# Differential attention on one core: the output tile is copied out of PSUM by ScalarE and normed in SBUF

## The chip, the cores and the metric

The kernel runs on one core of a Trainium2 chip. The core has five engines, each with a queue of its own that it works through in order: TensorE (PE in the profile, its weight loads PEld), VectorE (DVE), ScalarE (ACT), GpSimd (POOL) and SyncE (SP), which issues the DMAs. Matrix products are written to PSUM, eight banks of 2 KB in each of 128 partitions; everything else lives in SBUF. The metric is the device time of one execution in microseconds (us).

## The reference, cut to what matters

Four sandwiched layers are computed on x of 8 sequences of 512 tokens of 256 features, each as x = x + layernorm(layer(layernorm(x))): differential attention, a local transformer, token and channel diffusion, and a mixture of experts. Only the end of the first one is touched:

```python
attn = softmax(A1) - lam * softmax(A2)        # causal, 16 heads
O = einsum('bhnm,bhmd->bhnd', attn, V)
O = O / rms * rms_scale * (1.0 - LAMBDA_INIT)
Oc = O.transpose(0, 2, 1, 3).reshape(b, n, H * 2 * dh)
return Oc @ Wo.T                              # y
...
x = x + _layernorm(y, axis=-1)                # (y - mean) / sqrt(var + 1e-5)
```

The change concerns the last two lines: the product with Wo, its norm, and the addition to x.

## The kernel before, in words

The differential attention is the function `diff`, the first stage of the kernel. It works through 64 turns n: 8 sequences, 4 groups of 4 heads in each, and 2 softmaxes for each group. A turn has 8 slots, and the loop over slots at the end of `diff` writes the order of everything by hand:

- In each slot, TensorE makes a pair of score blocks `sc` (L355) for the row maxima of turn n, and a pair of transposed blocks `sa` (L365) for the exponentials of an earlier turn. The four products use different quarters of the array's rows and run together. VectorE adds a mask to `sc` (L368) and takes maxima into `spread` (L369); ScalarE makes the exponentials `e` from `sa` (L372); GpSimd masks one block of `e` in every second slot (L375, the selects).
- `lower` (slot 0): four transposes turn the maxima into `pm` (L288), and VectorE adds them to the queries `qT` (L380). The `sa` from slot 2 on need this `qT`.
- `divide` (slot 1): `pn` (L406) sums the exponentials, ScalarE makes the reciprocal `rec` (L408, L409), VectorE multiplies `oc` by it (L410); in every second turn VectorE joins the two softmaxes (L413) and GpSimd squares the result, `sq` (L415).
- `values` (slots 2 to 4): the products `po` with the values (L388), three additions of exponentials on GpSimd (L393), which together take some 7 us, and the copy of `po` to `oc` (L397, L399).
- `queries` and `keys` (slots 5 and 6 of every second turn), and `between()`, which does one part of the work waiting in a list: a sequence's `prepare`, a group's `heads` (`pr`, `rs`, and on GpSimd `oT`, L428), or a tile of a sequence's `finish`.

`finish` is what is changed. It has four tiles of 128 tokens, each done by one call of `between()`: `pp` is the product with Wo, in one PSUM bank; `self.norm` takes its statistics on VectorE (`st`, L184, and `mv`, L186), makes `rs` on GpSimd (L172, L173), and on VectorE makes `z` (L194); GpSimd adds `z` to `x` (L444). The tiles of one sequence fall into three successive turns: tile 0 at the end of the first, tiles 1 and 2 at the end of the second, tile 3 at the end of the third. `pp` shares a pool of two banks with most other products of the stage:

```python
psm, pse, ps = (pool(n, b, space=PSUM) for n, b in (("d_psm", 2), ("d_pse", 1), ("d_ps", 2)))
```

`pp`, `pm`, `pn`, `po`, `pr`, `pq`, `pk` and `pv` all take turns in the two banks of `d_ps`. So `pm` or `pn`, which follow `pp` at once, wait for the bank of a `pp` until its last reader has ended. `z` has two buffers in SBUF.

Of the kernel before, what the change touches and what calls it, by code (L numbers as in the profile page):

```python
# [120 lines left out]
class Net:  # L121
# [169 lines left out]
    def diff(self, nb):  # L291
# [4 lines left out]
        with ExitStack() as ctx:  # L296
            pool = lambda n, b, **k: ctx.enter_context(self.tc.tile_pool(name=n, bufs=b, **k))
            wk, small = pool("d_wk", 2), pool("d_small", 4)
            psm, pse, ps = (pool(n, b, space=PSUM) for n, b in (("d_psm", 2), ("d_pse", 1), ("d_ps", 2)))
            nc = self.nc  # L300
# [117 lines left out]
            def heads(m, oc, sq):  # L418

                b, r = divmod(m, 4)  # L420
                if r == 0:
                    outs[b] = wk.tile([P, 4, S], F32, name="oT", tag="oT")
                pr = ps.tile([P, S], F32, name="pr", tag="ps")
                self.mm(pr, [(self.const[:, C_B32:C_B32 + P], sq)])
                rs = wk.tile([P, S], F32, name="rs", tag="rs", bufs=1)
                nc.scalar.activation(rs, pr, AF.Ln, bias=column(C_EPS))
                nc.scalar.activation(rs, rs, AF.Exp, scale=-0.5)
                nc.gpsimd.tensor_mul(outs[b][:, r, :], oc, rs)  # L428
                if r == 3:
                    between.add(finish(b))  # L430
                return
                yield

            def finish(b):
                oT = outs.pop(b)
                for t in range(NT):
                    if t:
                        yield
                    pp = ps.tile([P, D], F32, name="pp", tag="ps")
                    self.mm(pp, [(oT[:, c, self.tok(t)], self.wo[:, c, :]) for c in range(4)])  # L440
                    z = wk.tile([P, D], F32, name="z", tag="z")
                    self.norm(small, [pp], [z])
                    xs = self.xb(b)[:, t, :]
                    nc.gpsimd.tensor_add(xs, xs, z)  # L444

# [1111 lines left out]
```

## Time and profile before

| | |
|---|---|
| median of 3 runs | 3858.41 us (3852.4 to 3862.06) |
| the profiled execution | 3852.22 us, of which the span 3850.4 us |
| mean granted TensorE clock | 0.955 of full speed |
| busy, share of the span | PE 90%, DVE 57%, ACT 48%, POOL 41% |
| the steady part of `diff`, 57 to 1146 us | 1089 us, PE busy 1027.9 us, POOL 716.0 us, granted clock 0.97 |
| `pp` read for the statistics (L184), 32 times | 0.43 us each |
| `z` from `pp` (L194), 32 times | 0.54 us each |

The span runs from the first to the last instruction. In the views an arrow reads "written from": `z<-pp,mv,rs` is the instruction that writes z from pp, mv and rs. A row of the timeline has its start, its length, engine, line, operation, operands, and in brackets how long the engine was idle before it and what it waited for. A group of like instructions that lie together is one row, marked x8 or the like.

### The profile page before, as it was taken

What the parts mean: (1) busy time and instruction counts of PE and PEld (TensorE: products, weight loads), DVE (VectorE), ACT (ScalarE), POOL (GpSimd) and SP (SyncE); (2) the same over time, 40 slices, a digit from 0 to 9 for tenths busy, and PEclk for the clock granted to TensorE, in tenths of its full rate; (3) what the DMA queues carried; (4) which work ended last, traced back from release to release, by engine and by line L of the source; (5) the groups of instructions that cost most, each with busy time, mean ns of one, the idle gap of its engine ahead of it and who ended that gap; (6) DMA issues with size and microseconds to landing.
All of it is one profiled execution on the core that took longest, in us unless ns stands there. A gap on an engine that the chain in (4) does not pass through costs nothing. (4 is left out here: it accounts for less than half of the span.)

```text
span 3850.4 us, 53540 instructions
## 1 busy us (share of the span) xinstructions
PE 3463.0 (90%) x20034; PEld 1885.2 (49%) x20034; DVE 2209.5 (57%) x4364; ACT 1840.8 (48%) x3687; POOL 1583.2 (41%) x1432
## 2 busy tenths in 40 slices
PE   8999999999987999999999999997988888679985
PEld 3344434343424556666666555564444444346554
DVE  6777767776646666665556666663244443344445
ACT  3555555555543444444444444453655555223334
POOL 3676666676654433333333333321012211153333
PEclk9999999999979999999999999998999999789997
DMA  9300000000001000000010000000000000421115
GB/s 343 124 1 7 7 6 1 7 6 1 6 6 34 4 4 4 4 4 25 4 31 12 9 9 9 9 20 23 1 23 23 23 17 17 146 70 53 52 44 166
DMA packets 95137, 130.28 MB, mean 34 GB/s; under 512 B 24702, under 2 KB 73242, under 8 KB 94874
## 3 DMA queue, kind: packets, MB, share of 16 engines
q1 hardware_dynamic: 88346, 108.94, 8.8%
q0 software_dynamic: 6528, 17.87, 1.3%
q8 instruction: 162, 2.65, 0.3%
q14 instruction: 101, 0.83, 0.1%
HBM read 57.40 MB, written 65.18 MB: 32 GB/s over the span
## 5 line engine op out<-in xcount | busy, mean ns | idle before, releaser
L372 ACT ACTIVATE e<-sa 128x1024 f32<-128x1024 f32 (+3 forms) x512 | 359.2, 702 | 337.3 <-PE sa L365 334.7
L393 POOL TENSOR_TENSOR e<-e,e 128x1536 f32<-128x1536 f32 (+2 forms) x192 | 451.6, 2352 | 92.4 <-PE po L388 82.5
L365 PE MATMUL sa<-qT,kT 32*128 32x512 f32 (+3 forms) x2048 | 430.0, 496 | 9.1 <-ACT e L372 8.8
L369 DVE TENSOR_REDUCE spread<-sc 128x2 f32<-128x256 f32 (+3 forms) x512 | 422.4, 825 | 15.6
L355 PE MATMUL sc<-kT,qT 32*128 32x128 f32 (+3 forms) x2048 | 420.3, 491 | 8.9 <-DVE spread L369 5.3
L655 ACT ACTIVATE lp<-lp,lnm 128x256 f32<-128x256 f32 (+1 forms) x512 | 240.1, 470 | 260.6 <-DVE lnm L647 156.2
L659 POOL TENSOR_TENSOR lp<-lp,lrs 128x1024 f32<-128x1024 f32 x64 | 121.1, 1893 | 528.8 <-DVE lrs L656 508.7
L1087 ACT ACTIVATE te<-tsa 128x1024 f32<-128x1024 f32 x256 | 249.0, 1024 | 136.6 <-PE tsa L1083 87.5
L368 DVE TENSOR_TENSOR sc<-sc,const 128x256 f32<-128x256 f32 x512 | 218.6, 427 | 158.6 <-PE sa L365 138.2
L355 PEld LDWEIGHTS sc<-kT,qT 32*128 32x128 f32 x2048 | 159.5, 188 | 282.9 <-issue 126.2
L213 PE MATMUL lpa<-ghT,lw 128*128 128x512 f32 x640 | 284.8, 600 | 12.1 <-ACT ghT L568 12.1
L213 PE MATMUL lqk<-qkv,lhT 128*128 128x512 f32 x512 | 247.8, 622 | 2.3 <-DVE qk L606 1.6
L607 POOL TENSOR_TENSOR qk<-qk,over 128x1024 f32<-128x1024 f32 x64 | 151.4, 2365 | 207.7 <-DVE qk L606 207.7
L375 POOL TENSOR_SCALAR_AFFINE_SELECT e<-e 128x512 f32<-128x512 f32 x256 | 160.4, 640 | 169.3 <-ACT e L372 169.3
L1406 ACT ACTIVATE ehT<-eht,enorm 128x128 f32<-128x128 f32 x288 | 108.2, 457 | 210.0 <-PE eht L1402 202.7
L213 PEld LDWEIGHTS lpa<-ghT,lw 128*128 128x128 f32 x640 | 119.4, 190 | 163.3 <-issue 136.3
L388 PE MATMUL po<-e,v 128*32 128x512 f32 (+3 forms) x2048 | 188.3, 451 | 4.0 <-POOL e L375 3.6
L644 DVE TENSOR_TENSOR lp<-lsc,const 128x768 f32<-128x768 f32 (+1 forms) x128 | 138.7, 1083 | 86.5 <-PE lsc L641 86.0
L641 PE MATMUL lsc<-lkT,lqT 64*128 64x256 f32 (+1 forms) x1024 | 156.6, 386 | 28.1 <-DVE qk L606 28.0
L365 PEld LDWEIGHTS sa<-qT,kT 32*128 32x128 f32 x2048 | 158.9, 189 | 43.4 <-ACT e L372 27.4
L1083 PE MATMUL tsa<-tqT,tkT 32*128 32x512 f32 x1024 | 171.0, 673 | 6.3 <-DVE tqT L1038 3.4
L213 PE MATMUL py<-ew,ehT 128*128 x576 | 145.2, 396 | 24.1 <-ACT ehT L1406 23.7
(293 smaller groups left out, 6799.5 us busy)
## 6 DMA issues: line engine op xcount, KB each, us to landing
xrows<-zero SPq DMA_DIRECT2D x66, 514.0 KB
ex<-xrows SPq DMA_DIRECT2D x72, 128.5 KB
ew<-in_L_ffn_w_dram SPq DMA_DIRECT2D x16, 512.0 KB
egot<-yrows SPq DMA_DIRECT2D x16, 512.0 KB
x<-in_L_attn_X_dram SPq DMA_DIRECT2D x8, 512.0 KB
saved<-x SPq DMA_DIRECT2D x8, 512.0 KB
lx<-saved SPq DMA_DIRECT2D x8, 512.0 KB
xf<-xf SPq DMA_DIRECT2D x8, 512.0 KB
```

Source lines behind the costliest of these rows:

```text
L213: self.nc.tensor.matmul(out, lhsT=l, rhs=r, start=i == 0, stop=i == len(pairs) - 1)
L355: nc.tensor.matmul(sc[:, i, :w], lhsT=qT[g, self.tok(t)], rhs=kT[g, :w], start=True, stop=True)
L365: nc.tensor.matmul(sa[:, i, :S - k * P], lhsT=kT[g, self.tok(k)], rhs=qT[g, k * P:], start=True, stop=True)
L368: nc.vector.tensor_add(sc[:, :, w - P:w], sc[:, :, w - P:w], own)
L369: nc.vector.tensor_reduce(self.spread[n % 2][:, t, g0:g0 + 2, 0 if n % 2 else 16], sc[:, :, :w], AX.X, ALU.max, negate=True)
L372: nc.scalar.activation(x[:, h0:h0 + 2, :], sa[:, :, :S - k * P], AF.Exp, scale=0.25)
L375: nc.gpsimd.affine_select(x[:, :, :P], x[:, :, :P], [[0, 4], [1, P]], ALU.is_ge, 0.0, base=0, channel_multiplier=-1)
L388: nc.tensor.matmul(pos[n][group(g), k * P:], lhsT=seqs[b][1][:, k, 4 * r + g, :], rhs=x[:, g, :], start=k == 0, stop=k == 2)
L393: nc.gpsimd.tensor_add(y, y, es.pop((n, k)))
L655: nc.scalar.activation(x, x, AF.Exp, bias=nm[:, i, k:k + 1], accum_out=rs[:, i, k:k + 1])
L1083: m = nc.tensor.matmul(sa[i // 2][:, i % 2, :], lhsT=kT[q, self.tok(k)], rhs=qT[q, :], start=True, stop=True)
L1087: nc.scalar.activation(e[:, 2 * i:2 * i + 2, :], sa[i], AF.Exp)
```

## The change

`finish` now copies `pp` to `z` on ScalarE. The norm then reads z and writes it in place, with the same instructions as before on VectorE and GpSimd. The bank's only reader is the copy.

```diff
                     z = wk.tile([P, D], F32, name="z", tag="z")
-                    self.norm(small, [pp], [z])
+                    nc.scalar.copy(z, pp)
+                    self.norm(small, [z], [z])
                     xs = self.xb(b)[:, t, :]
                     nc.gpsimd.tensor_add(xs, xs, z)
```

## The prediction

> **What bounds the kernel now.** I read, in this order: the table of windows, to see what the differential stage lacks; who waits for the tile z; and the timeline of one sequence's finish, twice.
>
> ```profile
> 57.00:1146.00 1089.00, 1027.94 (x7500) 428.88 (x7502) 747.43 (x1276) 591.70 (x913) 716.00 (x597) 0.97 0.08 29
> ```
>
> Columns: stretch, length, busy time of TensorE, its weight loads, VectorE, ScalarE, GpSimd; granted clock. TensorE is busy 1027.9 of 1089 us, so the stage runs at its pace: only TensorE's gaps and its clock (0.97, not 1) can be gained.
>
> ```profile
> who waited for it (us, times):
>   PEld pn L406: 28.0, 21
>   PE pn L406: 23.5, 21
>   POOL x L444: 21.1, 32
>   PEld pm L288: 9.0, 6
>   PE pm L288: 7.9, 6
> ```
>
> Of TensorE's gaps some 33 us are waits for z: pn 23.5 and pm 7.9 in TensorE's own rows, and 1.7 of pp's at the end. All come from the bank that pp holds until z is made. But such a sum is an upper bound: what is next late has to be looked up.
>
> Tiles 0 and 3 of each finish look like this (first sequence):
>
> ```profile
> 253.01 0.43 DVE L184 BATCH_NORM_STATS2 st<-pp 128x6 f32<-128x256 f32 x1 [0.77 <-PE pp L213]
> ...
> 254.91 0.54 DVE L194 TENSOR_SCALAR z<-pp,mv,rs 128x256 f32<-128x256 f32 x1 [0.58 <-POOL rs L173]
> 255.37 0.68 DVE L380 TENSOR_TENSOR qT<-qT,pm 128x512 f32<-128x512 f32 x1
> ...
> 255.50 1.07 PE L406 MATMUL pn<-e,const 128*32 128x512 f32 x8 [1.08 <-DVE z L194]
> ...
> 256.51 0.70 PE L365 MATMUL sa<-qT,kT 32*128 32x512 f32 x2
> ...
> 259.64 1.04 POOL L415 TENSOR_TENSOR sq<-oc 128x512 f32<-128x512 f32 x1 [2.79 <-DVE oc L413]
> ```
>
> The statistics start at 253.01, GpSimd makes rs, z ends at 255.45, and pn, which needs the bank, starts 1.07 us late. Behind z on VectorE stands qT (L380, ends 256.05), for which the next sa waits; and pn leads by rec and oc to sq, the start of GpSimd's next stretch. Tiles 1 and 2, a pass later:
>
> ```profile
> 260.64 7.20 POOL L393 TENSOR_TENSOR e<-e,e 128x1536 f32<-128x1536 f32 x3
> ...
> 268.98 1.27 POOL L428 TENSOR_TENSOR oT<-oc,rs 128x512 f32<-128x512 f32 x1
> ...
> 271.21 0.54 DVE L194 TENSOR_SCALAR z<-pp,mv,rs 128x256 f32<-128x256 f32 x1 [3.04 <-POOL rs L173]
> ...
> 271.81 0.33 PE L288 MATMUL pm<-const,spread 128*128 128x128 f32 x1 [1.32 <-DVE z L194]
> ...
> 272.12 0.69 DVE L369 TENSOR_REDUCE spread<-sc 128x2 f32<-128x512 f32 x1
> ...
> 272.88 0.90 PE L288 MATMUL pm<-const,spread 128*128 128x128 f32 x3 [0.74 <-DVE spread L369]
> ...
> 275.11 1.93 PE L406 MATMUL pn<-e,const 128*32 128x512 f32 x8 [0.59 <-DVE z L194]
> ...
> 276.99 1.22 PE L365 MATMUL sa<-qT,kT 32*128 32x512 f32 x2
> ```
>
> GpSimd runs without a gap from sq to oT and only then makes rs, so z waits 3.04 us, the maximum over scores (L369) stands behind z on VectorE, and TensorE idles for pm 1.32 us (the bank) and 0.74 us (the maximum). Then the clock is granted at half: pn takes 1.93 us here, 1.07 at tile 0; the pair sc and sa starts at 276.99 and po only at 279.00, 2.01 us later, against 1.06 at tile 0 (256.51 to 257.57).
>
> **The change, part by part.** Per tile one copy of 128x256 is added on ScalarE, 32 in all; bn_stats and the final tensor_scalar read SBUF instead of PSUM. Every engine's queue keeps its order, but for two places: the copy stands right behind the exponential of the slot before pp, and at tile 1 VectorE's sc add (L368) now stands ahead of z, not behind it.
>
> *The copy.* The page has none of 128x256. Bounds: the exponential of 128x256 from PSUM, 0.38 us, and the copy of 128x512, 0.58. I take 0.38, the same size. Behind it in ScalarE's queue waits the next exponential, behind that the next sa: but ScalarE idles 1.12 us (tile 0) and 1.43 and 1.76 us (tiles 1, 2) there, since sa is issued after pp. So the queue costs nothing; if that cover were gone, 0.38 x 32 = 12 us. The copy itself waits for pp and, as z has two buffers, for GpSimd's addition (L444) of the tile two before, which at tile 2 ended at 256.26, long ago. With two handovers of about 0.04 (pp's end 252.97 to the statistics 253.01) the statistics start 0.45 us later.
>
> *z and statistics from SBUF.* bn_stats: 0.41 (st<-x) against 0.43: nothing. The tensor_scalar: 0.41 in x<-x,mv,rs, 0.54 from PSUM; but h<-x,mv,rs, the same form, takes 0.40 to 1.36 while GpSimd adds. At z GpSimd has just made rs, and its next instruction waits for z, so it is idle: I take 0.41, a gain of 0.13; the upper end is 1.36.
> The Trainium skill, "SBUF — State Buffer", section "Who interferes with whom", speaks against the change here: a tensor_scalar in a 2-port mode and a GpSimd instruction exclude each other for a whole instruction. The spread of h agrees; if z always met such an instruction, the sum would be that of the slower rival below.
>
> *Tiles 0 and 3.* pn no longer waits, and starts 1.07 us earlier. But sa waits for qT: +0.45 - 0.13 makes its end 256.37 and sa 256.41 instead of 256.51. So of 1.07 us only 0.10 is left; the wait has moved from the bank to VectorE's queue. This holds for 12 tiles of sequences 0 to 5 and two of sequence 6.
> What else comes early is oc (L410, 257.93): rec no longer holds it, VectorE does: qT starts 0.32 later, then add (0.59), maximum (0.46) and its 0.43, so oc at 257.18, 0.75 earlier. So sq, the additions L393, the selects, oT and rs, back to back on GpSimd, move by 0.75.
>
> *Tile 1.* z at 270.46 instead of 271.21. From z's start to the maximum's was 0.91 us; the sc add between (0.46) now stands ahead, and z is 0.13 shorter: 0.32. The maximum starts at 270.78 instead of 272.12, and pm goes on 1.34 earlier, at 271.54. The bank itself is free long before. TensorE's idle time falls from 2.06 us to about 0.8 us. A gap of 1.07 at tile 0 leaves the clock whole, so I take it that 0.8 does.
>
> *Tile 2.* From the maximum to qT was 2.85 us on VectorE, now 2.72: qT 273.50 to 274.18, sa at 274.22 instead of 276.99. TensorE is ready before that: from pm's rest at 271.54 it is 0.48 to the next sc (as at full clock in sequence 1), 0.60 to pn and 1.0 for pn (as in turns with no finish beside): 273.62. So here too qT decides. At full clock po follows 1.06 us after sa, at 275.28 instead of 279.00: 3.72 us, and 0.15 more in the next slot (1.17 us against 1.0). So 3.87 us, tile 0 of this finish contained.
>
> *Sum.* The half clock lasts two windows (6.8 us) in sequences 0, 2, 4, 5 and one (3.4 us) in 1 and 3, where z of tile 1 to po takes 7.42 us instead of 7.79: 3.45 us there. 4 x 3.87 + 2 x 3.45 = 22.4. Tile 3, 6 x 0.10 = 0.6. Sequence 6: 2 x 0.10, and its last tile, where pm's rest (1066.05) hangs on two maxima behind z: z earlier by 0.75, add and z shorter by 0.59, so at 1064.5: 1.5. The last sequence, at the stage's end, has its four z in a chain with nothing beside: 4 x 0.13 less, one hop of 0.45 more: 0.1. Together 24.8 us. Later slots follow at the pace they have now, so nothing gives it back. The profiled execution took 3852.2 us, 6.2 under the median of the runs: 3827.4, in terms of the median 3833.6. I say 3833.
>
> **Rivals.**
> *The half clock stays.* It would, if its windows come from the low load around pm rather than from the 2.06 us. Then pm's rest costs 0.90 from 271.54 on, sc follows at 272.36, pn at 273.2, sc and sa at 275.05, po at 277.06 instead of 279.00: 1.94 x 6 = 11.6, with the other 2.4 us 14 us: 3844. For it: some idle time remains. Against: the half clock comes in each of these six places and after none of the gaps of 1.07 us.
> The Trainium skill, "TensorE: Matmul & The Clock Gate", section "Part 1: The HAM clock gate", gives a free-running window of about 3.4 us, and idleness of a whole window as what halves the clock; by that rule the gaps here would not be the cause and this rival would hold. The trace differs: 2.06 us in two parts were enough.
>
> *The wait only moves.* GpSimd's stretch does not move (oc held by something else) and the maximum stays behind a z that waits for rs: then TensorE starts each slot as before. About 3856. For it: tiles 0 and 3, where just that is forecast. Against: at tile 1 the sc add leaves z's shadow anyway.
>
> *Slower: z becomes the slow one.* Place: z in VectorE's queue ahead of qT. Price: at 1.36 us instead of 0.41, sa starts 0.85 late at 14 tiles (12 us), the four z of the end cost 3.8 more, and of the six turns perhaps 0.8 each is left (5 us): +11, 3869. It decides from about 1.1 us for z. Against it: GpSimd waits for z at that time.
>
> **How the numbers follow.** Forecast 0.70, half clock 0.15, moved wait 0.09, slower 0.06. About 0.3% (11.6 us) can be told from no change. The forecast and most of the second rival are beyond it: faster 0.80. The third and the rest of the second: same 0.14. Slower 0.06. The range takes in the runs' own spread of 5 us to either side below the forecast, more if GpSimd's stretch moves by the whole 1.07, and reaches past the second rival: 3821 to 3848.
>
> **What would show it.** Right: copies of about 0.38 us; z about 0.41 us; no wait of pn or pm for z in TensorE's rows; sa of tiles 0 and 3 released by qT; rs of tile 1 some 0.7 us earlier after sq; pn at tile 2 near 1.07 us; granted clock of the stage up. Wrong: z over 0.8 us, pn still 1.9 us at tile 2, or sq as late as before.

## The result, and the profile after

The changed kernel takes 3839.99 us in the median of 5 runs (3830.72 to 3844.74) against 3858.41 us (3852.4 to 3862.06) before; the ratio is 0.9948, 95% interval 0.9935 to 0.9961. The execution that was profiled took 3837.43 us, its span 3835.7 us, against 3852.22 and 3850.4. So the change gains, with 18.4 us in the medians and 14.8 us between the profiled executions, where 24.8 us were forecast.

The first view is who waited for z and for whatever made it, of the changed kernel; the rows of pn and pm that stood here before are gone, and nothing of TensorE waits for z any more.

```profile
L442 ACT COPY z<-pp x32: 372/372/373, 261.9 to 1155.9; 128x256 f32<-128x256 f32 x32
L184 DVE BATCH_NORM_STATS2 st<-z x32: 415/427/432, 262.3 to 1157.1; 128x6 f32<-128x256 f32 x32
L194 DVE TENSOR_SCALAR z<-z,mv,rs x32: 411/412/415, 264.1 to 1158.9; 128x256 f32<-128x256 f32 x32
...
who waited for it (us, times):
  DVE st L184: 38.4, 24
  POOL x L445: 16.9, 32
  ACT z L442: 3.8, 2
```

The three numbers behind a colon are the shortest, median and longest in ns. The copy takes 0.372 us and z 0.412 us, each time. What waits now is the statistics for the copy.

Tile 0 in the timeline of the changed kernel (everything here stands 8.93 us later than in the profile before, since this execution reached the first pp that much later, with the same instructions ahead of it):

```profile
261.94 0.37 ACT L442 COPY z<-pp 128x256 f32<-128x256 f32 x1 [0.63 <-PE pp L213]
262.35 0.43 DVE L184 BATCH_NORM_STATS2 st<-z 128x6 f32<-128x256 f32 x1 [1.17 <-ACT z L442]
...
263.29 1.06 PE L406 MATMUL pn<-e,const 128*32 128x512 f32 x8
...
264.14 0.41 DVE L194 TENSOR_SCALAR z<-z,mv,rs 128x256 f32<-128x256 f32 x1 [0.58 <-POOL rs L173]
264.47 0.68 DVE L380 TENSOR_TENSOR qT<-qT,pm 128x512 f32<-128x512 f32 x1
...
265.30 1.13 PE L365 MATMUL sa<-qT,kT 32*128 32x512 f32 x4
```

pn has no wait in brackets. But qT still stands behind z on VectorE, and sa starts 5.39 us after pp (259.91), against 5.53 before. Tiles 1 and 2 in the same timeline:

```profile
279.15 0.41 DVE L194 TENSOR_SCALAR z<-z,mv,rs 128x256 f32<-128x256 f32 x1 [1.53 <-POOL rs L173]
279.48 0.69 DVE L369 TENSOR_REDUCE spread<-sc 128x2 f32<-128x512 f32 x1
...
280.22 0.55 PE L288 MATMUL pm<-const,spread 128*128 128x128 f32 x3 [0.74 <-DVE spread L369]
...
281.13 1.07 PE L406 MATMUL pn<-e,const 128*32 128x512 f32 x8
...
283.05 1.13 PE L365 MATMUL sa<-qT,kT 32*128 32x512 f32 x4
284.11 1.06 PE L388 MATMUL po<-e,v 128*32 128x512 f32 x8
```

The maximum (L369) follows z at once, since the mask is already added; TensorE idles 0.74 us at pm instead of 1.32 + 0.74; pn takes 1.07 us instead of 1.93; po starts 24.20 us after the finish's first pp, where it was 28.02 us in the kernel before. In all six finishes the changed kernel has 24.17 to 24.20 us here, the kernel before 27.39 to 28.02.

And yet the stage's row in the table of windows shows no better clock:

```profile
57.00:1130.00 1073.00, 1045.43 (x7491) 434.61 (x7490) 742.22 (x1280) 603.34 (x939) 714.68 (x595) 0.96 0.08 29
```

On the same stretch the kernel before had 0.97. The half clock has left the finishes and turned up elsewhere: 13.7 us of it ahead of the first finish, where nothing was changed (3.4 us before; none in the second trace of the changed kernel, below), more of the stage's end, where both kernels have it, now lies within the row, and there is some in the turn behind tile 3. The last is new. Here is that turn in the changed kernel, after the first finish and after the second, and then in the kernel before, after the first:

```profile
311.09 0.70 PE L365 MATMUL sa<-qT,kT 32*128 32x256 f32 x4 [0.85 <-ACT e L372]
...
313.09 0.69 PE L288 MATMUL pm<-const,spread 128*128 128x128 f32 x2
...
314.45 1.85 PE L406 MATMUL pn<-e,const 128*32 128x512 f32 x8
```

```profile
445.39 0.70 PE L365 MATMUL sa<-qT,kT 32*128 32x256 f32 x4 [0.85 <-ACT e L372]
...
447.21 0.44 PE L288 MATMUL pm<-const,spread 128*128 128x128 f32 x2
...
448.18 1.07 PE L406 MATMUL pn<-e,const 128*32 128x512 f32 x8
```

```profile
306.19 0.70 PE L365 MATMUL sa<-qT,kT 32*128 32x256 f32 x4 [0.85 <-ACT e L372]
...
308.00 0.44 PE L288 MATMUL pm<-const,spread 128*128 128x128 f32 x2
...
308.98 1.06 PE L406 MATMUL pn<-e,const 128*32 128x512 f32 x8
```

The same wait of 0.85 us for an exponential, then the same short products. In the changed kernel pn takes 1.85 us in one place and 1.07 in the other. The kernel before has this wait too, with the clock at full behind all six.

What that costs is read from one finish's first pp to the next one's. Before: 137.02, 136.23, 136.58, 136.12, 135.82 us. After: 134.32, 132.56, 132.57, 136.08, 133.11. The two of 132.56 and 132.57 have no half clock at all; the one of 136.08 has 6.8 us of it in the turn behind tile 3 and 3.4 us a turn later, those of 134.32 and 133.11 have 3.4 us.

### The profile page after: what moved, and what is told of

It reads as the page before. It is cut to its first block, busy times and chain, and to the rows that moved or that the text cites. A ratio compares the mean times of both kernels' runs of the same rounds, so it can differ in the third digit from the quotient of the medians.

```text
span 3835.7 us, 53567 instructions
## 1 busy us (share of the span) xinstructions
PE 3484.9 (91%) x20034; PEld 1894.1 (49%) x20034; DVE 2201.1 (57%) x4364; ACT 1855.1 (48%) x3719; POOL 1583.6 (41%) x1432
## 5 line engine op out<-in xcount | busy, mean ns | idle before, releaser
L369 DVE TENSOR_REDUCE spread<-sc 128x2 f32<-128x256 f32 (+3 forms) x512 | 422.2, 825 | 15.3
```

What stands on the lines that cost most here:

```text
L369: nc.vector.tensor_reduce(self.spread[n % 2][:, t, g0:g0 + 2, 0 if n % 2 else 16], sc[:, :, :w], AX.X, ALU.max, negate=True)
```

## The experiments

Ratios are to the kernel before, run beside each kernel on the same chip; the chips of the three groups (first four, next four, last four runs) differ by up to 0.8% in the time of the kernel before, so only ratios are compared. Three times are read from each trace. A: from pp of tile 0 to the sa of the next turn's slot 2, the first that needs the new qT. B: from pp of tile 0 to po behind tile 2. C: from pp of tile 3 to po behind it.

| kernel | ratio, 95% interval | A | B | C |
|---|---|---|---|---|
| before | 1 | 5.53 | 27.39 to 28.02 | 6.59 |
| changed | 0.9948 (0.9935 to 0.9961) | 5.38 | 24.17 to 24.20 | 6.49 |
| the same again | 0.9955 (0.9941 to 0.9970) | 5.38 | 24.17 to 24.20 | 6.49 |
| copy that nothing reads | 1.0024 (1.0015 to 1.0034) | 5.83 | 25.85 to 27.45 | 6.88 |
| copy, statistics from the bank | 0.9959 (0.9947 to 0.9972) | 5.38 | 24.18 to 24.20 | 6.50 |
| z issued late | 0.9906 (0.9891 to 0.9921) | 4.40 | 23.12 to 24.77 | 5.51 |
| statistics, then copy | 0.9978 (0.9966 to 0.9989) | 5.08 | 25.55 to 26.59 | 6.13 |
| bank held, rs on ScalarE | 0.9920 (0.9905 to 0.9935) | 5.10 | 22.81 | 6.16 |
| copy, and rs on ScalarE | 0.9898 (0.9883 to 0.9913) | 4.40 | 21.44 | 5.51, once 5.79 |
| GpSimd addition, done early | 0.9964 (0.9950 to 0.9978) | 5.38 | 24.17 to 24.21 | 6.49 |
| wait behind tile 3 filled | 0.9946 (0.9926 to 0.9966) | 5.38 | 24.17 to 24.20 | 6.49 |
| GpSimd at work at z | 1.0008 (0.9992 to 1.0024) | 5.38 | 25.70 to 26.65 | 6.50 |
| copy, rs on ScalarE, wait filled | 0.9874 (0.9857 to 0.9891) | 4.40 | 21.44 | 5.51, once 5.79 |
| copy on VectorE | 0.9890 (0.9868 to 0.9912) | 4.39 | 23.16 | 5.44 |

**The changed kernel again.** No edit.

> The changed kernel once more, nothing else. Theory (short chain on VectorE and GpSimd in the turn of tiles 1 and 2, and no half clock there): the way from the first pp of a finish to the first po after its tile 2 is 28.0 us before and 24.2 us in the changed kernel; here again 24.2 (within 0.1) in all six full sequences, and 18 to 25 us less in all. If the half-clock windows that the changed kernel shows in turns without a finish (3.4 us at 313, 849 and 982 us, 6.8 at 712 us) are a matter of where the free-running window falls, they lie elsewhere this time. If they are the change's doing, they lie at the same turns again.

A, B and C were the same to 0.03 us; the half clock lay in the turn behind tile 3 of five finishes (all but the fourth; in the first trace behind the first, fourth, fifth and sixth), and in none of the finishes. So that it falls in this turn is not an accident of one execution, while the finishes behind which it falls change from one to the next. The whole was 17.1 us shorter than before in the medians, just under the 18 to 25 us expected.

**A copy that nothing reads.** The hop without the release of the bank:

```diff
+                    spare = wk.tile([P, D], F32, name="spare", tag="spare")
+                    nc.scalar.copy(spare, pp)
                     self.norm(small, [pp], [z])
```

> The kernel before with ScalarE's copy added, but the copy goes to a tile that nobody reads: norm and z read the bank as before, so only the copy's cost is left. Theory: the copies (0.37 us, 32 of them) lie in ScalarE's idle time, the way from pp to po stays 28.0 us, total within 3 us of before. Rival, ScalarE's queue matters: up to 12 us slower. Rival, the gain came from a shifted order of instructions and not from the bank: this one gains too.

It came out slower, 3869.02 against 3859.39 us in the medians, outside the 3 us expected and within the rival's 12. The timeline of this kernel shows one reason:

```profile
259.28 0.37 ACT L443 COPY spare<-pp 128x256 f32<-128x256 f32 x1 [0.63 <-PE pp L213]
259.69 0.43 DVE L184 BATCH_NORM_STATS2 st<-pp 128x6 f32<-128x256 f32 x1 [1.17 <-ACT spare L443]
```

The statistics read pp, not the copy, and still wait for ScalarE: two engines' reads of one bank are put one behind the other. So the hop of 0.41 us is paid here, though nothing reads the copy, and A grows by 0.30 (5.83 against 5.53). The Trainium skill, "PSUM — Partial Sum Buffer", section "PSUM bank collisions raise a hardware error", says that reads against reads of one bank collide too and that the compiler orders them; the row agrees.

The 9.6 us are not all the hop's, and B isn't comparable. TensorE's order changed as well: between tiles 0 and 1 it waits 1.80 us for a maximum, pp of tile 1 comes 16.3 to 17.8 us after that of tile 0 instead of 14.5, and by then GpSimd has caught up, so that z of tile 1 waits 0.64 us for rs instead of 3.04, and pm waits for nothing, although the bank is held. So this run gives no clean price of the copy, and doesn't settle whether another order alone could gain.

**Copy on ScalarE, statistics from the bank.** Only z from the copy:

```diff
-                    self.norm(small, [z], [z])
+                    self.normed([z], [z], *self.moments(small, [pp]))
```

> The changed kernel, but the statistics read the bank beside the copy, and only the last step reads the copy: the bank is held by the longer of two reads, and the copy is out of the chain to qT. Theory (tiles 0 and 3 are bound by qT behind z on VectorE): the hop of 0.45 us is gone, sa of tile 0 follows pp's start 0.4 us sooner than in the changed kernel (5.39 there), the way to po is 23.8, and the whole is 4 to 7 us faster than the changed kernel. Rival (the bank alone was the matter): the same as the changed kernel.

No difference to the changed kernel, for the same reason: the statistics have the row "[1.17 <-ACT z L442]" here too, so that the hop was not taken out. The run decides nothing on the hop's price, and the 4 to 7 us expected did not come.

**z issued late.** The last instruction of the norm, and the addition to x, are issued after the next turn's `lower`:

```diff
-                    self.norm(small, [z], [z])
-                    xs = self.xb(b)[:, t, :]
+                    late.append((z, self.xb(b)[:, t, :], self.moments(small, [z])))
...
+            def flush():
+                while late:
+                    z, xs, m = late.pop(0)
+                    self.normed([z], [z], *m)
...
+                if j == 1:
+                    flush()
```

> The changed kernel, but z (the last step of the norm) and the addition to x are issued after the next lower() instead of at once, so that qT doesn't stand behind z on VectorE at tiles 0, 2 and 3; at tile 1 z still stands ahead of the maximum. Theory: sa of tile 0 follows as soon as TensorE is ready, about 1.0 us sooner than in the changed kernel; likewise at tile 3 and at tile 2; the way to po is 22.8 to 23.3 us; in all 12 to 18 us faster than the changed kernel. Rival (the bank alone): as the changed kernel.

A and C fell by 0.98 us each and the ratio to 0.9906; in the medians it is 22.6 us under the changed kernel run again beside it (3819.62 and 3842.26 us), more than the 12 to 18 us expected. B met the 22.8 to 23.3 us expected in three finishes; in the other three half clock began in the finish, and it is 24.71 to 24.77. In the turn behind tile 3 this trace has no half clock. In the timeline VectorE does qT first:

```profile
257.34 0.68 DVE L380 TENSOR_TENSOR qT<-qT,pm 128x512 f32<-128x512 f32 x1
...
258.26 0.45 DVE L194 TENSOR_SCALAR z<-z,mv,rs 128x256 f32<-128x256 f32 x1
```

This shows what held sa at tiles 0 and 3: qT behind z in VectorE's queue, and z behind rs, just as the prediction read it.

**Statistics first, then the copy.** The statistics are issued ahead of the copy, so that the copy waits for them and not they for it:

```diff
+                    mv, rs = self.moments(small, [pp])
                     nc.scalar.copy(z, pp)
-                    self.norm(small, [z], [z])
+                    self.normed([z], [z], mv, rs)
```

> The statistics read the bank as in the kernel before, then ScalarE copies pp to z, and z is normed in SBUF. Same work and same early release as the changed kernel, but the copy no longer stands ahead of the statistics, so the hop of 0.45 us is out of the chain to qT. Theory (in tiles 0 and 3 the chain pp, statistics, rs, z, qT decides): from pp to the first sa 5.38 - 0.42 = about 4.95 us, tile 3 from pp to po 6.49 - 0.42 = about 6.05 us; at tile 1 z is made ahead of the addition of the mask again, which costs some 0.4 us there, while GpSimd's stretch is 0.4 earlier, so the way from tile 0 to po of tile 2 stays at 24.2. Total 3 to 6 us under the changed kernel, ratio to the kernel before 0.993 to 0.995. Rival (ScalarE's copy, now later, ends behind z's statistics and rs, or pn waits for it): the same times as the changed kernel, pp to sa 5.4.

A and C fell by 0.30 and 0.36 us (0.42 expected), but B rose to 25.55 to 26.59, and the kernel gains less than the changed one (ratio 0.9978, where 0.993 to 0.995 was expected). The cause is the place that was expected to cost 0.4 us: in VectorE's order the mask's addition stands behind z again.

```profile
275.40 0.41 DVE L194 TENSOR_SCALAR z<-z,mv,rs 128x256 f32<-128x256 f32 x1 [2.67 <-POOL rs L173]
275.73 0.43 DVE L368 TENSOR_TENSOR sc<-sc,const 128x256 f32<-128x256 f32 x1
...
276.94 0.55 PE L288 MATMUL pm<-const,spread 128*128 128x128 f32 x3 [1.63 <-DVE spread L369]
...
278.75 1.94 PE L406 MATMUL pn<-e,const 128*32 128x512 f32 x8
```

TensorE idles 1.63 us for the maximum, and half clock is back in all six finishes. The bank is free early here, as in the changed kernel. So it is not the bank alone that brought the gain at tiles 1 and 2: without the mask's addition ahead of z, 1.4 to 2.4 of the 3.8 us of B are gone.

**Bank held, rs on ScalarE.** The kernel before, with rs made by a logarithm and an exponential on ScalarE (the switch `logs` that the kernel's other layers use):

```diff
+                    self.logs = True
                     self.norm(small, [pp], [z])
+                    self.logs = False
```

> The kernel before, with the bank held until z, but rs is made on ScalarE by a logarithm and an exponential instead of on GpSimd. It tells whether what the change gained at tiles 1 and 2 comes from the bank, or could as well be had by not letting rs stand behind oT on GpSimd. Theory 1 (the bank): pm at tile 1 and pn at tiles 0 and 3 still wait for z, though less; the way from tile 0 to po of tile 2 stays between 26 and 28 us, ratio 0.997 to 1.000. Theory 2 (the late rs): z of tile 1 is there some 3 us earlier, pm waits for nothing, the half clock leaves the finish, and the way is 24 us or less, ratio at or below 0.995. I hold the second for the likelier, as z waited 3.04 us for rs at tile 1 against 0.58 at tile 0.

The second theory holds: B is 22.81 us in all six, less than with the copy, and the ratio 0.9920, though pp holds its bank until z.

```profile
270.62 0.20 ACT L170 ACTIVATE rs<-rs 128x1 f32<-128x1 f32 x1
...
270.86 0.54 DVE L194 TENSOR_SCALAR z<-pp,mv,rs 128x256 f32<-128x256 f32 x1 [0.18 <-ACT rs L170]
271.07 1.26 POOL L428 TENSOR_TENSOR oT<-oc,rs 128x512 f32<-128x512 f32 x1
...
272.50 0.66 PE L288 MATMUL pm<-const,spread 128*128 128x128 f32 x4
```

At tile 1 z starts 0.21 us before GpSimd begins oT, and ends 1.1 us before pm starts. What held the bank so long there was rs behind oT in GpSimd's queue; the bank was only where that was seen. The run doesn't separate this from VectorE's order, which changed with it: qT stands ahead of z at tiles 0 and 3 here, and the mask's addition ahead of z at tile 1. pn still waits 0.65 us behind tiles 0, 2 and 3, now for qT, the reader of pm.

**Copy, and rs on ScalarE.** The same two lines around the norm of the changed kernel.

> The changed kernel with rs made on ScalarE too. In the order of VectorE's instructions qT then stands ahead of z at tiles 0 and 3, and the maximum ahead of z at tile 1, as in the run that issued z late. If the place of qT behind z is what limits the changed kernel in tiles 0 and 3: pp to sa 4.4 us, tile 3 from pp to po 5.5 us, way to po of tile 2 at most 23.2 us; total 18 to 26 us under the changed kernel, ratio 0.988 to 0.991. If two more instructions on ScalarE (0.2 to 0.3 us each, ahead of an exponential for which TensorE waits) cost as much as they bring: 0.992 or above.

As expected: A 4.40, C 5.51 in five finishes and 5.79 in one, B 21.44, ratio 0.9898. The two instructions on ScalarE cost nothing that shows. z itself took 0.405 to 0.884 us here, 0.794 in the median, as it meets a select or oT on GpSimd; it stands behind qT, or at tile 1 behind the maximum, and hinders nobody.

**GpSimd beside z, first attempt.** One addition on GpSimd more for each tile, to a tile that nothing reads:

```diff
+                    mv, rs = self.moments(small, [z])
+                    spare = wk.tile([P, D], F32, name="spare", tag="spare")
+                    nc.gpsimd.tensor_add(spare, xs, xs)
+                    self.normed([z], [z], mv, rs)
```

> The changed kernel with one more GpSimd instruction behind rs in each tile: an addition of 128x256 to a tile that nothing reads. It runs while VectorE norms z, which in the changed kernel meets an idle GpSimd. It puts my rival of a slow z to the test. If GpSimd at work lengthens z as it lengthens the other tensor_scalars that read SBUF (0.40 to 1.36 us): z at 0.8 to 1.4 us, pp to sa 5.8 to 6.3 us, and the kernel 6 to 14 us slower than the changed one, ratio 0.997 to 1.000. If z keeps to 0.41 us: pp to sa 5.4 us, and only x comes later, which nothing soon waits for: within 3 us of the changed kernel, ratio about 0.995.

The addition needs nothing but x, and all 32 of them stand in the first 43 us of the span, far from z. So this says nothing on a slow z, and serves as one more run of the changed kernel's finish: A, B and C are those of the changed kernel, the ratio 0.9964.

**The wait behind tile 3 filled.** In the slot of that wait, once per sequence:

```diff
+                if fill:
+                    pf = ps.tile([P, S], F32, name="pf", tag="ps")
+                    for i in range(2):
+                        nc.tensor.matmul(pf[:, :D], lhsT=self.const[:, C_B32:C_B32 + P], rhs=sqs[-1][:, :D], start=True, stop=True)
...
```

> The changed kernel; in the turn after tile 3 of each finish TensorE waits 0.85 us for an exponential (L372). Into that wait this kernel puts two products of 128x256, a repeat of work already done, that nothing reads (about 0.5 us, six times). So far half clock came in that turn only where a clock window of 3.41 us ended 1.50 us or more behind the end of the wait (17 of 17 such gaps in the runs of the changed kernel and of its variants), and in none where it ended earlier. Theory 1 (the wait, together with the short products behind it, makes the low window, and where it ends is chance): with the wait filled the turn is at full clock in all six, wherever a window ends; the granted clock of the stage goes from 0.96 to 0.98, and each turn saved is worth 1.2 to 3.5 us, together 3 to 8 us under the changed kernel. Theory 2 (the short products of 128 columns alone are what halves the clock): the half clock stays in those turns whose window ends late, and the time is that of the changed kernel within 2 us.

(The count and the 1.50 us in that text are wrong. A clock window is read here from the granted clock: all half clock starts on a grid of 3.41 us. In the eleven traces in which all six waits are of 0.85 us, half clock began at the first end of a window behind the wait in 34 of 34 cases where that end lay 1.36 to 2.99 us behind it. In none of the other 32 did it: in 29 the end lay 0.01 to 1.23 us behind the wait, and in 3, at 3.36 to 3.41 us, the window began only with the wait's end.)

```profile
307.42 1.13 PE L361 MATMUL pf<-sq,const 128*128 128x256 f32 x4
308.48 0.70 PE L371 MATMUL sa<-qT,kT 32*128 32x256 f32 x4
...
311.27 1.07 PE L412 MATMUL pn<-e,const 128*32 128x512 f32 x8
```

The wait is gone (pf takes 1.13 us, not 0.5, and sa starts 0.14 us later), and the turn is at full clock in all six. In this run and in the one below with the same filling, a window ended 1.54 to 3.08 us behind the start of this sa in 7 of 12 turns, in six of them between 1.36 and 2.99 us; none of the seven fell to half clock. Theory 1 holds: wait and short products together, and where the window ends. The granted clock of the stage is 0.98. The gain is smaller than expected: 664.35 us from the first finish to the sixth, against 668.64 and 672.15 in the two traces of the changed kernel and 667.29 in the one above, and the ratio, 0.9946, cannot be told from that kernel's.

**GpSimd at work at z, second attempt.** The extra instruction now reads mv and rs:

```diff
+                    nc.gpsimd.tensor_scalar(spare, xs, mv[:, 0, 0:1], rs[:, 0:1], ALU.subtract, ALU.mult)
```

> As the last run with GpSimd at work beside z, but its extra instruction (a tensor_scalar of 128x256 to a tile that nothing reads) now needs rs, so that it can't be done early, and starts when z does. If GpSimd lengthens a z that reads SBUF (0.80 us instead of 0.41 was seen beside a select in the run with rs on ScalarE): z 0.7 to 1.4 us, pp to sa 5.7 to 6.4 us instead of 5.38, and 6 to 14 us slower than the changed kernel, ratio 0.998 to 1.001. If not: z 0.41 us and pp to sa 5.4.

The total is as the first case had it, but not by its mechanism: z kept to 0.413 us and A to 5.38. What it costs is seen at tiles 1 and 2:

```profile
278.81 0.41 DVE L194 TENSOR_SCALAR z<-z,mv,rs 128x256 f32<-128x256 f32 x1 [2.04 <-POOL rs L173]
278.88 1.35 POOL L446 TENSOR_SCALAR spare<-x,mv,rs 128x256 f32<-128x256 f32 x1
...
279.88 0.33 PE L288 MATMUL pm<-const,spread 128*128 128x128 f32 x1 [1.26 <-DVE spread L369]
...
282.59 0.41 DVE L194 TENSOR_SCALAR z<-z,mv,rs 128x256 f32<-128x256 f32 x1 [1.64 <-POOL rs L173]
```

GpSimd's 1.35 us push its whole row of work: at tile 1 rs and so z wait 2.04 us instead of 1.53, pm 1.26 instead of 0.74, and at tile 2 z waits 1.64 us for rs instead of 0.61. B is 25.70 us where the clock stays whole and up to 26.65 where half clock falls into the finish. B makes up most of what is lost: the five steps are 13.0 us longer than in the first trace of the changed kernel, 9.8 of it in B. So an rs that comes 0.5 us later at tile 1 and 1.0 us later at tile 2, with the half clock that this brings back, goes far to undo the gain (1.0008). The run doesn't show where the rest goes.

**Both improvements together.** rs on ScalarE, and the wait filled.

> Both improvements together: rs on ScalarE, as in the run with copy and rs on ScalarE, and the wait of the turn after tile 3 filled. Times within a finish as in that run (4.4, 21.4 and 5.5 us); no half clock in the turn after tile 3. If the two add up, 3 to 6 us under that run: ratio 0.988 to 0.9895.

0.9874 is the lowest ratio of all, just under the 0.988 to 0.9895 expected, but its interval overlaps that of the kernel without the filling, so the filling's gain isn't shown. In four of the twelve turns of the two kernels with the filling half clock came about 19 us after the place filled, in the next turn, so that part of what is saved is lost again.

**The copy on VectorE.**

```diff
-                    nc.scalar.copy(z, pp)
+                    nc.vector.tensor_copy(z, pp)
```

> The changed kernel with the copy on VectorE instead of ScalarE. VectorE's order then puts qT ahead of z at tiles 0 and 3 and z behind no mask; the copy costs VectorE itself some 0.4 us ahead of the statistics, about what the hop over ScalarE cost. Should be as the run that issued z late: pp to sa 4.4 to 4.8 us, tile 3 from pp to po 5.5 to 5.9 us, way to po of tile 2 at most 24.8 us; ratio 0.990 to 0.993. If the 0.4 us per tile on VectorE are on the path: 0.994 or above.

Better than expected: 0.9890. The copy costs VectorE 0.425 us, about the hop over ScalarE, and VectorE's order now has qT ahead of z (A 4.39), as in the run that issued z late:

```profile
261.48 0.66 DVE L380 TENSOR_TENSOR qT<-qT,pm 128x512 f32<-128x512 f32 x1
262.52 0.71 DVE L194 TENSOR_SCALAR z<-z,mv,rs 128x256 f32<-128x256 f32 x1 [0.39 <-POOL rs L173]
```

With as short an edit it gains about twice what the change gained.

## Why the prediction was right, point by point

The time was forecast as 3833, range 3821 to 3848, and is 3840; faster by over 0.3% had 0.80. The finishes went as forecast; one step of the sum, that nothing is given back behind them, did not.

- *The copy*: taken at 0.38, measured 0.372, hidden on ScalarE. Right.
- *The hop*: 0.45 forecast, 0.41 in the rows (start of the copy to start of the statistics). But only 0.30 of it reached z at tile 0 (264.14 - 8.93 = 255.21 against 254.91), since mv now follows the start of the statistics by 0.66 us instead of 0.77. bn_stats took 0.427 where 0.41 was taken from another row.
- *z from SBUF*: 0.412, forecast 0.41.
- *Tiles 0 and 3*: sa gained 0.15 instead of 0.10 at tile 0 and 0.10 at tile 3 (C 6.59 to 6.49). That the numbers are so near is in part luck: qT ended 0.15 us sooner than forecast (256.22 against 256.37), and sa followed its end by 0.15 us instead of 0.04. That the wait moves from the bank to qT behind z was read from the order before the run, and the late z showed it.
- *Tile 1*: the maximum 1.34 us earlier and TensorE's idle time 0.8. In the first finish: maximum at 279.48 - 8.93 = 270.55, against 272.12 before, 1.57 earlier; idle 0.74. GpSimd's sq came 1.01 us earlier (267.56 - 8.93 = 258.63 against 259.64), not 0.75.
- *Tile 2 and the sum*: 28.02 became 24.20; 3.72 was forecast, 3.82 came. From the first finish to the sixth, five finishes, 3 x 3.87 + 2 x 3.45 + 5 x 0.10 = 19.0 us were forecast. The steps free of half clock behind tile 3 are 132.56 (four of them) and, for the last, 131.75 in the trace with the early GpSimd additions: 662.0 against 681.8 before, so 19.8.
- *The step that failed* is the sentence "Later slots follow at the pace they have now, so nothing gives it back", and with it "granted clock of the stage up". The five steps took 668.6, not 662.0: 6.6 us were given back to half clock in the turn behind tile 3 and the one after it (134.32 - 132.56, 136.08 - 132.56 and 133.11 - 131.75); in the second trace of the changed kernel it was 10.2 (672.15). The wait that makes that turn vulnerable was in the profile before, but there, in the one trace, the clock window always ended 0.37 to 1.05 us behind it. Before, a step of some 136.4 us is nearly 40 windows (40 x 3.413 = 136.5), so the window ends at about the same place in each finish; with 132.6 us it does not, and in four of six it ended late enough. Of the 24.8 us forecast these 6.6 had to be taken off. The time lies in the range all the same because the range was wide enough, not because the step was foreseen. The profiled executions differ by 14.8 us: 8.9 later at the first pp, which no changed instruction precedes (2.8 in the second trace of the changed kernel, so chance), 13.1 gained in the five steps, 6.6 from the sixth finish to the stage's last z (236.94 to 230.38 us; 5.8 forecast), and 3.9 behind the stage, which the change doesn't touch.
- *Rival, half clock stays*: not in these six places, as the rows of pn show. But its idea that low load around short products brings it about is right in the turn behind tile 3: there 0.85 us of wait suffices, less than the gap of 1.07 us that the prediction named as harmless at tile 0. The prediction's argument "a gap of 1.07 at tile 0 leaves the clock whole, so 0.8 does" gave the right answer for tile 1 from too little: the gap's length alone doesn't decide. The answer itself was not luck of the windows: in the 30 finishes of the five traces with the changed kernel's order, a window ended 0.54 to 2.79 us behind the wait of some 0.74 us at pm, and half clock came in none.
- *Rival, the wait only moves*: that is what happened at tiles 0 and 3, as forecast. At tile 1 a part of it stayed: the maximum still stands behind a z that waits for rs (1.53 us instead of 3.04), and TensorE still idles 0.74 us for it.
- *Rival, z becomes the slow one*: z stayed at 0.41 in the changed kernel. Its mechanism exists (up to 0.884 beside a select or oT): the price seen is up to 0.47 us and not 0.95, and a z below 1.1 us would not have decided, by the prediction's own estimate. No run has z beside GpSimd's additions. The kernel that does lose the gain keeps z at 0.41 and has rs late. The Trainium skill, "SBUF — State Buffer", section "Who interferes with whom", lets issue order decide who blocks; that fits z at 0.41 when it started 0.07 us ahead of GpSimd's instruction, but not the z that started 0.02 us ahead of a select and took 0.80 (copy, and rs on ScalarE).

What the prediction didn't weigh is that the same gain was to be had elsewhere: at tile 1 the bank was held because rs stood behind oT, and with rs on ScalarE no copy is needed.

## What to carry to other kernels

When an engine waits for a buffer, ask why its last reader is late before giving the buffer an earlier last reader: here, at tile 1, the reader waited for a tiny instruction that stood behind other work in another engine's queue, and moving that tiny instruction to a third engine gained more than the copy (0.9920 against 0.9948). After taking a wait away, look in the order of each engine for what stood behind it: a one-line edit moved qT and the mask's addition to other places, and that order was worth about as much as the change itself (0.9890 against 0.9948). And where TensorE is nearly full, a time saved shifts everything after it against the windows of the clock, so look for weak places that had been lucky until now.

## What the runs showed of the hardware

- Half clock starts on one grid of 3.41 us in each of the 14 traces. A wait of 0.85 us with short products behind it (128 columns) brought half clock in 34 of 34 cases when the window ended 1.36 to 2.99 us behind the wait, and in 0 of 32 when it ended sooner or began only with the wait's end. With products in place of the wait it came in none of 7 late windows. The Trainium skill, "TensorE: Matmul & The Clock Gate", section "Part 1: The HAM clock gate", has the window free-running with 3413 ns, which agrees; its table of the clock's two states names an idle window as the condition, and here 0.85 us of idleness in one, with short products behind it, was enough. What load is the limit, no run here shows. One turn later half clock came in some traces too; why, no run here shows.
- z from PSUM took 0.535 to 0.545 us in all 32 cases of the kernel that holds the bank and has rs on ScalarE, 28 of them beside work on GpSimd; z from SBUF took 0.41 us with GpSimd idle, and 0.41 to 0.88 with it at work. Here the slower source was the steadier one.
- The copy on ScalarE and the statistics on VectorE, where both read pp's bank, never ran side by side: the second waited for the first, whichever order the program gave them (0.41 us from start to start with the copy first, 0.47 with the statistics first).
